# A graph network's attention: weighted rows, row maxima and a comparison counter held in PSUM

## The chip, the cores and the metric

The kernel runs as one program on one core of a Trainium2 chip. The metric is device time in microseconds (us), from start to end of one execution. Engines are named as in the profile: PE (matrix products), PEld (its weight loads), DVE (vector), ACT (scalar), POOL (which here issues indirect gathers) and SP (which issues plain transfers). SBUF is the large on-chip memory, PSUM the small one into which PE writes.

## What is computed

A node matrix x (6250 x 128) passes two residual blocks over a graph of 200,000 edges that are sorted by destination. The first block is a stack of five attention layers:

```python
def _gat_layer(x, src, dst, ea, W, We, a_src, a_dst, a_edge, b, n):
    h = x @ W
    e = ea @ We
    s = (h @ a_src)[src] + (h @ a_dst)[dst] + e @ a_edge
    s = jax.nn.leaky_relu(s, NEG_SLOPE_ATT)
    smax = jax.ops.segment_max(s, dst, num_segments=n)
    ex = jnp.exp(s - jax.lax.stop_gradient(smax)[dst])
    denom = jax.ops.segment_sum(ex, dst, num_segments=n)
    alpha = ex / denom[dst]
    out = jax.ops.segment_sum(h[src] * alpha[:, None], dst, num_segments=n)
    return out + b
...
h = jnp.maximum(_layernorm(x, axis=-1), 0.0)
x = x + _L0_gnn_ref(h, edge_index, edge_attr_16, ...)
h = jnp.maximum(_layernorm(x, axis=-1), 0.0)
x = x + _L1_gnn_ref(h, src, dst, ...)
```

Every node has a self-loop too, and between the layers there is some mixing. The second block is an edge convolution: rows of both ends of each edge are gathered, multiplied, normalised over all edges twice, and averaged per destination. The degrees of the nodes, by destination and by source, are counted as well.

## The kernel before

The edges are laid out in rows of four (K = 4) with one destination each. 128 rows make a group q; four groups (GQ = 4) make a tile of 16 columns of 128 edges. The nodes lie in 49 buckets of 128.

In order of time the kernel sorts and counts (0 to about 460 us in the profiled execution), builds edge records (L477, to about 1205), runs five attention layers (about 1259 to 14685), gathers for the edge convolution (L786, 15203 to 17639), and does the rest of that convolution.

One attention layer is `attention(l)` (L562). `heads` multiplies the nodes by the layer's weights and writes a table in HBM with a node's 128 features, a one, and its source score. Then a loop of 109 tiles calls `some`:

1. POOL issues 16 indirect gathers (L591), each of 128 table rows, into g, which has four buffers. SP loads neq (zero where a row's destination is a given node of the bucket) and eqt (the transposed match).
2. t (L602) is the gathered score plus the edge's own, tk (L604) the maximum over a row's four edges, and z (L607) is tk spread over the nodes of the bucket with a large negative number where they don't match. PE transposes z into xp (L610); tm (L611) is the maximum per node.
3. A chain of small DVE instructions (L615 to L625) makes the running maxima TS, the scores u and m, and cor, the factor by which sums so far are rescaled. `three` (L213 to L216) splits the maximum in three bf16 pieces in R6, and PE brings them back to the edge rows as me (L632); am (L634) adds the pieces up, v (L636 to L638) is the score less the maximum, and ACT's ex (L640) its exponential.
4. y is the weighted sum of a row's four gathered rows, one for each of the four groups j: ACT multiplies the first (L644) and DVE multiplies and adds the other three (L646), each reading and writing y in SBUF.
5. oh (L648, ACT) is the match. PE adds the rows of y to their nodes as op (L652), and DVE rescales the node sums hb and adds op (L655), in a bucket that is looked up in registers that `regs` loads on DVE.

In every fifth tile a step of `count` (L187) adds to the degree: two compares on DVE of a counter 0..127 with edge numbers, ol (L193) and oo (L195), and products on PE in po. It reads the counter as iotab, in bf16 in SBUF. The degree by destination is counted so in the sort too.

A Tile framework places buffers, adds the waits and decides the order of instructions within each engine's queue; the engines take their queues in order. A tile's y sums stand behind the t of two tiles later in DVE's queue. PSUM is eight banks: po takes 1, xp 2, me 2 and op 3.

Of the kernel before, what the change touches and what calls it, by code (L numbers as in the profile page):

```python
# [9 lines left out]
F32 = mybir.dt.float32  # L10
# [10 lines left out]
P = 128  # L21
# [10 lines left out]
def gnn_kernel(ctx: ExitStack, tc: tile.TileContext, x, src, dst, ea, Ws, Wes, a_srcs, a_dsts, a_edges,  # L32
# [134 lines left out]
    with tc.tile_pool(name="gat", bufs=1) as gp:  # L167
# [18 lines left out]

        def count(to, lo, hi, sw, pp, c0=0, c1=CE):  # L187

            po = pp.tile([P, NB], F32, name="po", bufs=1)
            for c in range(c0, c1, G):  # L190
                n = min(G, c1 - c)
                ol = sw.tile([P, G, P], BF, name="ol", bufs=2)
                nc.vector.tensor_tensor(ol[:, :n], mid_bc(iotab, n, P), last_bc(lo[:, c:c + n], n, P), OP.is_equal)  # L193
                oo = sw.tile([P, G, NB], BF, name="oo", bufs=2)
                nc.vector.tensor_tensor(oo[:, :n], mid_bc(iotab[:, :NB], n, NB), last_bc(hi[:, c:c + n], n, NB), OP.is_equal)  # L195
                for j in range(n):
                    nc.tensor.matmul(po, ol[:, j, :], oo[:, j, :], start=(c + j == c0), stop=(c + j == c1 - 1))
                yield
            nc.vector.tensor_tensor(to, to, po, OP.add)
# [362 lines left out]
        def attention(l):  # L562

            with tc.tile_pool(name="nod", bufs=1) as lp, tc.tile_pool(name="nodp", bufs=2, space=PSUM) as pp:
                nc.scalar.dma_start(ael[:, :K * QM], ae_d[l, :, :K * QM])
                if l:
                    heads(l, lp, pp)
                nc.vector.tensor_tensor(nod[:, 1, :], nod[:, 1, :], aeloop[:, :, l], OP.add)

                for k, to in ((0, adE), (1, t0E)):  # L570
                    tp = pp.tile([NB, P], F32, name="ntp")
                    nc.tensor.transpose(tp, nod[:, k, :], ident)
                    nT = lp.tile([NB, P], F32, name="nT", bufs=2)
                    nc.scalar.copy(nT, tp)
                    for c in range(0, Q, 512):
                        n = min(512, Q - c)
                        ps = pp.tile([P, 512], F32, name="ep")
                        nc.tensor.matmul(ps[:, :n], nT, tboh[:, c:c + n], start=True, stop=True)
                        nc.scalar.copy(to[:, c:c + n], ps[:, :n])
                rem = lp.tile([P, Q], F32, name="rem")  # L580
                three(R6[:, :, 0:3], adE, rem)
                nc.vector.memset(TS[:, 0:1], -BIG)

            with tc.tile_pool(name="edg", bufs=2) as ep, tc.tile_pool(name="edgp", bufs=2, space=PSUM) as pp:
                steps = count(outdeg, slo, shi, ep, pp, CE * l // L, CE * (l + 1) // L)

                def some(q0, n):
                    c0 = K * q0
                    g = ep.tile([P, G, HW], F32, name="g", bufs=4)
                    for j in range(G):  # L590
                        nc.gpsimd.indirect_dma_start(  # L591
                            out=g[:, j, :], out_offset=None, in_=table,
                            in_offset=bass.IndirectOffsetOnAxis(ap=srci[:, c0 + j:c0 + j + 1], axis=0))
                    neq = ep.tile([P, GQ, P], BF, name="neq", bufs=4)
                    nc.sync.dma_start(neq, neq_d[q0 // GQ])
                    eqt = ep.tile([P, GQ, P], BF, name="eqt", bufs=4)
                    nc.sync.dma_start(eqt, eqt_d[q0 // GQ])
                    r = regs(0, q0, GQ, DVE, (NB - 1) * HW)

                    t = ep.tile([P, GQ, K], F32, name="t")  # L600
                    tf = t.rearrange("p q k -> p (q k)")
                    nc.vector.tensor_tensor(tf, g[:, :, D + 1], ael[:, c0:c0 + G], OP.add)  # L602
                    tk = ep.tile([P, GQ], F32, name="tk")
                    nc.vector.tensor_reduce(tk, t, AX.X, OP.max)  # L604
                    tm = ep.tile([P, GQ], F32, name="tm")
                    z = ep.tile([P, GQ, P], F32, name="z")
                    nc.vector.scalar_tensor_tensor(z, neq, -BIG, last_bc(tk, GQ, P), op0=OP.mult, op1=OP.add)  # L607
                    xp = pp.tile([P, GQ, P], F32, name="xp", bufs=2)
                    for j in range(GQ):
                        nc.tensor.transpose(xp[:, j, :], z[:, j, :], ident)  # L610
                    nc.vector.tensor_reduce(tm, xp, AX.X, OP.max)  # L611

                    sl = slice(q0, q0 + GQ)
                    t0, ad, rst = t0E[:, sl], adE[:, sl], reset[:, sl]
                    nc.vector.tensor_tensor(tm, tm, t0, OP.max)  # L615
                    nc.vector.tensor_tensor_scan(TS[:, q0 + 1:q0 + 1 + GQ], rst, tm, TS[:, q0:q0 + 1], OP.add, OP.max)
                    u = ep.tile([P, 2, GQ], F32, name="u")
                    nc.vector.tensor_tensor(u[:, 0, :], TS[:, sl], rst, OP.add)
                    nc.vector.tensor_tensor(u[:, 0, :], u[:, 0, :], t0, OP.max)
                    nc.vector.tensor_tensor(u[:, 0, :], u[:, 0, :], ad, OP.add)  # L620
                    nc.vector.tensor_tensor(u[:, 1, :], TS[:, q0 + 1:q0 + 1 + GQ], ad, OP.add)
                    m = ep.tile([P, 2, GQ], F32, name="m")
                    nc.vector.scalar_tensor_tensor(m, u, SLOPE_ATT, u, op0=OP.mult, op1=OP.max)  # L623
                    cor = ep.tile([P, GQ], F32, name="cor")
                    nc.vector.tensor_tensor(cor, m[:, 0, :], m[:, 1, :], OP.subtract)  # L625
                    nc.scalar.activation(cor, cor, AF.Exp)
                    tmp = ep.tile([P, GQ], F32, name="tmp")
                    three(R6[:, sl, 3:6], m[:, 1, :], tmp)

                    me = pp.tile([P, GQ, 6], F32, name="me", bufs=2)  # L630
                    for j in range(GQ):
                        nc.tensor.matmul(me[:, j, :], eqt[:, j, :], R6[:, q0 + j, :], start=True, stop=True)  # L632
                    am = ep.tile([P, GQ, 2], F32, name="am")
                    nc.vector.tensor_reduce(am, me.rearrange("p g (a b) -> p g a b", b=3), AX.X, OP.add)  # L634
                    v = ep.tile([P, GQ, K], F32, name="v")
                    nc.vector.tensor_tensor(v, t, last_bc(am[:, :, 0], GQ, K), OP.add)  # L636
                    nc.vector.scalar_tensor_tensor(v, v, SLOPE_ATT, v, op0=OP.mult, op1=OP.max)
                    nc.vector.tensor_tensor(v, v, last_bc(am[:, :, 1], GQ, K), OP.subtract)  # L638
                    ex = ep.tile([P, GQ, K], F32, name="ex")
                    nc.scalar.activation(ex, v, AF.Exp)  # L640

                    y = ep.tile([P, GQ, D + 1], F32, name="y")
                    for j in range(GQ):
                        nc.scalar.activation(y[:, j, :], g[:, K * j, :D + 1], AF.Identity, bias=zeroc, scale=ex[:, j, 0:1])  # L644
                        for k in range(1, K):
                            nc.vector.scalar_tensor_tensor(y[:, j, :], g[:, K * j + k, :D + 1], ex[:, j, k:k + 1], y[:, j, :], op0=OP.mult, op1=OP.add)  # L646
                    oh = ep.tile([P, GQ, P], F32, name="oh")
                    nc.scalar.activation(oh, neq, AF.Identity, bias=onec, scale=-1.0)  # L648
                    for h in range(0, GQ, 2):
                        op = pp.tile([P, 2, D + 1], F32, name="op", bufs=3)  # L650
                        for j in (h, h + 1):
                            nc.tensor.matmul(op[:, j - h, :], oh[:, j, :], y[:, j, :], start=True, stop=True)  # L652
                        for j in (h, h + 1):
                            a = hbf[:, ds(r[j], D + 1)]
                            nc.vector.scalar_tensor_tensor(a, a, cor[:, j:j + 1], op[:, j - h, :], op0=OP.mult, op1=OP.add)  # L655

                    if q0 % (5 * GQ) == 0 and q0 < QM:
                        next(steps, None)

                over(GQ, some, lambda: nc.scalar.dma_start(ael[:, K * QM:], ae_d[l, :, K * QM:]))  # L660
                for _ in steps:
                    pass
# [304 lines left out]
```

## Time and profile before

| | us |
|---|---|
| median of 9 runs | 18727.85 (18688.21 to 18760.27) |
| profiled execution | 18761.08 |
| its span | 18759.3 |
| attention layer 0, from POOL's first gather to its last | 2579.5 |
| layer 1 | 2582.9 |
| layer 2 | 2591.1 |
| layer 3 | 2595.7 |
| layer 4 | 2597.1 |
| edge convolution's gathers | 2436 |

Between two layers' gathers lie 101 to 133 us, in which the output of the one and the table of the next are made.

The engines' busy time over the span:

```profile
PE 4505.0 (24%) x24113; PEld 3280.7 (17%) x24113; DVE 7165.9 (38%) x23773; ACT 2826.5 (15%) x5544; POOL 10656.0 (57%) x10984
```

Each entry is busy us, the share of the span, and the number of instructions. No engine is busy for more than 57% of the span. A line of a group gives the kernel's line, the engine and its operation, output and inputs, the count, then busy us and mean ns of one, then the idle time of the engine before these instructions and what ended most of it. "issue" means that nothing visible was waited for; "remote" is a wait whose releaser isn't named. A line of a timeline gives start and length in us, the instruction, and in brackets the idle time before it.

### The profile page before, as it was taken

What the parts mean: (1) busy time and instruction counts of PE and PEld (TensorE: products, weight loads), DVE (VectorE), ACT (ScalarE), POOL (GpSimd) and SP (SyncE); (2) the same over time, 40 slices, a digit from 0 to 9 for tenths busy, and PEclk for the clock granted to TensorE, in tenths of its full rate; (3) what the DMA queues carried; (4) which work ended last, traced back from release to release, by engine and by line L of the source; (5) the groups of instructions that cost most, each with busy time, mean ns of one, the idle gap of its engine ahead of it and who ended that gap; (6) DMA issues with size and microseconds to landing.
All of it is one profiled execution on the core that took longest, in us unless ns stands there. A gap on an engine that the chain in (4) does not pass through costs nothing. (4 is left out here: it accounts for less than half of the span.)

```text
span 18759.3 us, 107717 instructions
## 1 busy us (share of the span) xinstructions
PE 4505.0 (24%) x24113; PEld 3280.7 (17%) x24113; DVE 7165.9 (38%) x23773; ACT 2826.5 (15%) x5544; POOL 10656.0 (57%) x10984
## 2 busy tenths in 40 slices
PE   4111111121111221111211111211111222222498
PEld 4011111111111111111111111111111111111268
DVE  7333333343333343333433333433333421221378
ACT  1111111111111111111101111111111111111267
POOL 1657666656666556666466666566666356565300
PEclk6555555555555555555555555555555555555699
DMA  3122222222222222222222222222222222222475
GB/s 101 56 58 56 56 56 58 56 60 57 57 57 56 53 61 56 56 56 56 59 55 56 55 56 57 57 56 55 56 57 56 67 89 88 87 90 88 144 252 201
DMA packets 717072, 1361.76 MB, mean 73 GB/s; under 512 B 223808, under 2 KB 486880, under 8 KB 673632
## 3 DMA queue, kind: packets, MB, share of 16 engines
q0 software_dynamic: 348800, 702.54, 16.1%
q1 hardware_dynamic: 338828, 616.20, 10.0%
q10 hardware_dynamic: 28756, 35.62, 0.6%
q8 instruction: 215, 3.52, 0.1%
q14 instruction: 473, 3.87, 0.1%
HBM read 1144.99 MB, written 208.56 MB: 72 GB/s over the span
## 5 line engine op out<-in xcount | busy, mean ns | idle before, releaser
L591 POOL DMA_INDIRECT g<-table,srci x8720 | 8491.6, 974 | 4987.5 <-issue 4387.9
L652 PE MATMUL op<-y,oh 128*128 128x129 f32 x4360 | 1598.0, 488 | 5708.2 <-DVE y L646 4151.4
L646 DVE SCALAR_TENSOR_TENSOR y<-g,ex,y 128x129 f32<-128x129 f32 x6540 | 1954.8, 348 | 2108.1 <-DVE y L646 784.0
L786 POOL DMA_INDIRECT g<-btable,srci x1744 | 1645.3, 943 | 1309.2 <-DVE xe L800 566.9
L652 PEld LDWEIGHTS op<-y,oh 128*128 128x128 f32 x4360 | 1071.7, 314 | 6230.5 <-issue 3751.3
L648 ACT ACTIVATE oh<-neq,onesq 128x512 f32<-128x512 bf16 x545 | 392.9, 721 | 5483.1 <-PE op L652 3540.5
L655 DVE SCALAR_TENSOR_TENSOR hb<-hb,cor,op 128x129 f32 x2180 | 756.5, 347 | 1153.7 <-remote 606.2
L804 DVE COPY xs<-xps 128x512 f32<-128x512 f32 x436 | 301.3, 691 | 2202.7 <-remote 1718.4
L803 PE MATMUL xps<-ident,xe 128*128 128x128 f32 x1744 | 467.3, 422 | 2158.6 <-DVE xe L800 1710.5
L610 PE MATMUL xp<-ident,z 128*128 128x128 f32 x2180 | 594.2, 428 | 1460.1 <-DVE am L634 367.9
L644 ACT ACTIVATE y<-g,zeroc,ex 128x129 f32<-128x129 f32 x2180 | 899.3, 483 | 19.0 <-DVE m L623 0.6
L632 PE MATMUL me<-R,eqt 128*128 128x6 bf16 x2180 | 135.5, 167 | 3055.6 <-DVE tk L604 1341.9
L477 POOL DMA_INDIRECT rg<-rec_d,rowi x436 | 472.6, 1084 | 559.8 <-DVE ix L470 272.9
L640 ACT ACTIVATE ex<-v 128x16 f32<-128x16 f32 x545 | 117.5, 216 | 4365.1 <-DVE v L638 1398.4
L803 PEld LDWEIGHTS xps<-ident,xe 128*128 128x128 f32 x1744 | 307.8, 214 | 2303.6 <-issue 2284.1
L632 PEld LDWEIGHTS <-eqt 128*128 128x128 bf16 x2180 | 106.3, 105 | 3211.6 <-issue 3209.8
L610 PEld LDWEIGHTS xp<-ident,z 128*128 128x128 f32 x2180 | 389.9, 217 | 1536.1 <-issue 1331.4
L806 ACT ACTIVATE sq<-xps 128x512 f32<-128x512 f32 x436 | 260.3, 597 | 2527.2 <-DVE xs L804 2238.9
L607 DVE SCALAR_TENSOR_TENSOR z<-neq,tk 128x512 f32<-128x512 bf16 x545 | 380.5, 698 | 478.2 <-remote 299.4
L611 DVE TENSOR_REDUCE tm<-xp 128x4 f32<-128x512 f32 x545 | 374.7, 688 | 322.0 <-remote 164.6
L602 DVE TENSOR_TENSOR t<-g,ael 128x16 f32<-128x16 f32 x545 | 100.1, 184 | 840.2 <-DMA g<-table,srci 719.9
L896 PE MATMUL rps<-fs,e 128*128 128x128 f32 x3488 | 409.1, 276 | 4.6 <-ACT e L889 4.6
(315 smaller groups left out, 8241.1 us busy)
## 6 DMA issues: line engine op xcount, KB each, us to landing
g<-table,srci POOLq DMA_INDIRECT x8720
e_d<-xs SPq DMA_DIRECT2D x109, 1024.0 KB
x<-e_d SPq DMA_DIRECT2D x109, 1024.0 KB
e<-e_d SPq DMA_DIRECT2D x109, 1024.0 KB
neq<-neq_d SPq DMA_DIRECT2D x654, 128.0 KB
eqt<-eqt_d SPq DMA_DIRECT2D x654, 128.0 KB
g<-btable,srci POOLq DMA_INDIRECT x1744
table<-hb SPq DMA_DIRECT2D x5, 3185.0 KB
```

Of the source, the lines that this page charges most:

```text
L477: nc.gpsimd.indirect_dma_start(out=rg[:, j, :, :].rearrange("p k r -> p (k r)"), out_offset=None, in_=rec_d, in_offset=bass.IndirectOffset ...
L591: nc.gpsimd.indirect_dma_start(out=g[:, j, :], out_offset=None, in_=table, in_offset=bass.IndirectOffsetOnAxis(ap=srci[:, c0 + j:c0 + j + ...
L607: nc.vector.scalar_tensor_tensor(z, neq, -BIG, last_bc(tk, GQ, P), op0=OP.mult, op1=OP.add)
L610: nc.tensor.transpose(xp[:, j, :], z[:, j, :], ident)
L644: nc.scalar.activation(y[:, j, :], g[:, K * j, :D + 1], AF.Identity, bias=zeroc, scale=ex[:, j, 0:1])
L646: nc.vector.scalar_tensor_tensor(y[:, j, :], g[:, K * j + k, :D + 1], ex[:, j, k:k + 1], y[:, j, :], op0=OP.mult, op1=OP.add)
L648: nc.scalar.activation(oh, neq, AF.Identity, bias=onec, scale=-1.0)
L652: nc.tensor.matmul(op[:, j - h, :], oh[:, j, :], y[:, j, :], start=True, stop=True)
L655: nc.vector.scalar_tensor_tensor(a, a, cor[:, j:j + 1], op[:, j - h, :], op0=OP.mult, op1=OP.add)
L786: nc.gpsimd.indirect_dma_start(out=g[:, j, :], out_offset=None, in_=btable, in_offset=bass.IndirectOffsetOnAxis(ap=srci[:, c0 + j:c0 + j + ...
L803: nc.tensor.transpose(ps[:, k, :], xe[:, k, :], ident)
L896: nc.tensor.matmul(ps[:, k, :], es[:, K * q + k, :], fs, start=True, stop=True)
```

## The change

Three things that DVE and ACT read and write lie in PSUM instead of SBUF, and the eight banks are shared out anew.

- `count` copies the counter into PSUM once per call (six calls), in f32 beside po, and both compares read that copy.
- tk lies in PSUM, in one tile mt together with me. mt has one buffer; me had two, in PSUM, and tk two, in SBUF.
- The weighted rows grow in yp, a PSUM tile for two groups j with two buffers: ACT writes the first product there, DVE adds the second and third there, and the fourth step writes the sum to y in SBUF, which PE reads as before. Both groups' ACT steps come ahead of the DVE steps of the pair.
- op has two buffers instead of three. The banks are then po with the counter 1, mt 1, xp 2, yp 2 and op 2.

```diff
-            po = pp.tile([P, NB], F32, name="po", bufs=1)
+            po = pp.tile([P, 2, P], F32, name="po", bufs=1)
+
+            io, po = po[:, 0, :], po[:, 1, :NB]
+            nc.vector.tensor_copy(io, iota)
...
-                nc.vector.tensor_tensor(ol[:, :n], mid_bc(iotab, n, P), last_bc(lo[:, c:c + n], n, P), OP.is_equal)
+                nc.vector.tensor_tensor(ol[:, :n], mid_bc(io, n, P), last_bc(lo[:, c:c + n], n, P), OP.is_equal)
...
-                nc.vector.tensor_tensor(oo[:, :n], mid_bc(iotab[:, :NB], n, NB), last_bc(hi[:, c:c + n], n, NB), OP.is_equal)
+                nc.vector.tensor_tensor(oo[:, :n], mid_bc(io[:, :NB], n, NB), last_bc(hi[:, c:c + n], n, NB), OP.is_equal)
...
-                    tk = ep.tile([P, GQ], F32, name="tk")
+                    mt = pp.tile([P, GQ + 6 * GQ], F32, name="mt", bufs=1)
+                    tk = mt[:, :GQ]
...
-                    me = pp.tile([P, GQ, 6], F32, name="me", bufs=2)
+                    me = mt[:, GQ:].rearrange("p (g a) -> p g a", a=6)
...
-                    for j in range(GQ):
-                        nc.scalar.activation(y[:, j, :], g[:, K * j, :D + 1], AF.Identity, bias=zeroc, scale=ex[:, j, 0:1])
-                        for k in range(1, K):
-                            nc.vector.scalar_tensor_tensor(y[:, j, :], g[:, K * j + k, :D + 1], ex[:, j, k:k + 1], y[:, j, :], op0=OP.mult, op1=OP.add)
+                    for h in range(0, GQ, 2):
+                        yp = pp.tile([P, 2, D + 1], F32, name="yp", bufs=2)
+                        for j in (h, h + 1):
+                            nc.scalar.activation(yp[:, j - h, :], g[:, K * j, :D + 1], AF.Identity, bias=zeroc, scale=ex[:, j, 0:1])
+                        for j in (h, h + 1):
+                            for k in range(1, K):
+                                nc.vector.scalar_tensor_tensor(y[:, j, :] if k == K - 1 else yp[:, j - h, :], g[:, K * j + k, :D + 1], ex[:, j, k:k + 1],
+                                                               yp[:, j - h, :], op0=OP.mult, op1=OP.add)
...
-                        op = pp.tile([P, 2, D + 1], F32, name="op", bufs=3)
+                        op = pp.tile([P, 2, D + 1], F32, name="op", bufs=2)
```

The number of instructions per tile stays the same on each engine.

## The prediction

> **What bounds the kernel now.** I read the costliest groups first, then the windows, then the timelines. Five attention layers fill most of the span, and in each layer POOL issues 109 tiles of 16 indirect gathers (L591).
>
> ```profile
> L591 POOL DMA_INDIRECT g<-table,srci x8720 | 8491.6, 974 | 4987.5 <-issue 4387.9
> L786 POOL DMA_INDIRECT g<-btable,srci x1744 | 1645.3, 943 | 1309.2 <-DVE xe L800 566.9
> L646 DVE SCALAR_TENSOR_TENSOR y<-g,ex,y 128x129 f32<-128x129 f32 x6540 | 1954.8, 348 | 2108.1 <-DVE y L646 784.0
> L655 DVE SCALAR_TENSOR_TENSOR hb<-hb,cor,op 128x129 f32 x2180 | 756.5, 347 | 1153.7 <-remote 606.2
> ```
>
> POOL is the floor: 0.94 us of work and 0.30 us of issue make 1.25 us per gather, 20 us per tile. The layers' windows, from POOL's first gather to its last, are 2579.5, 2582.9, 2591.1, 2595.7 and 2597.1 us, 12946 us together; 8720 gathers at 1.25 us are 10900. So 2046 us lie above the floor. POOL's timeline shows what most of them are:
>
> ```profile
> 7004.81 0.94 POOL L591 DMA_INDIRECT g<-table,srci  x1 [0.30 <-issue]
> ...
> 7021.33 0.94 POOL L591 DMA_INDIRECT g<-table,srci  x1 [10.58 <-issue]
> ...
> 7025.26 1.80 POOL L591 DMA_INDIRECT g<-table,srci  x1 [0.30 <-issue]
> ...
> 7117.36 0.94 POOL L591 DMA_INDIRECT g<-table,srci  x1 [14.71 <-issue]
> ```
>
> POOL runs bursts and then stops, because the fourth buffer of g is not free: its last reader is a y sum (L646) on DVE. DVE is busy for only 8.5 us per tile (925.8 us in the second layer's window, over 109), so it is not short of work capacity; it waits. Its timeline shows how:
>
> ```profile
> 7090.66 0.17 DVE L623 SCALAR_TENSOR_TENSOR m<-u 128x8 f32<-128x8 f32 x1 [1.23 <-DVE u L620]
> 7092.07 0.16 DVE L625 TENSOR_TENSOR cor<-m 128x4 f32<-128x4 f32 x1 [1.24 <-DVE m L623]
> ...
> 7096.26 0.16 DVE L615 TENSOR_TENSOR tm<-tm,t0E 128x4 f32<-128x4 f32 x1 [1.24 <-DVE tmp L214]
> 7097.66 0.17 DVE L215 CAST R<-tmp 128x4 bf16<-128x4 f32 x1 [1.24 <-DVE tm L615]
> ...
> 7116.27 0.35 DVE L646 SCALAR_TENSOR_TENSOR y<-g,ex,y 128x129 f32<-128x129 f32 x1
> ...
> 7118.90 3.38 DVE L646 SCALAR_TENSOR_TENSOR y<-g,ex,y 128x129 f32<-128x129 f32 x12
> ...
> 7124.49 0.16 DVE L619 TENSOR_TENSOR u<-u,t0E 128x4 f32<-128x4 f32 x1
> ```
>
> For much of a burst each DVE instruction that needs the one before it starts 1.24 us after that one's end (call this the late stretch). Some 5 to 8 us after POOL stopped, it is over: the twelve y sums at 7118.90 run without a gap, the sum at 7116.27 frees the buffer, and POOL resumes 1.1 us later. In the late stretch, casts and four-element adds wait as long as the wide sums.
>
> **The change, part by part.** The sums are made against the profiled execution (18761.1 us, span 18759.3), which is 33 us (0.2%) above the median of 18727.9; I carry the differences over to the median. 0.2% is also about what a measurement of this kernel can tell from no change.
>
> *Counter in PSUM.* Six copies of 128 elements, near 0.2 us each (L602, 16 elements, takes 184 ns), are 1 us. The compares L193 and L195 take 2288 and 976 ns from a bf16 counter. L512, which compares 2048 elements with the f32 counter, takes 2282 ns. So f32 costs nothing; a PSUM operand costs nothing in L655 against L646 (347 and 348 ns, same shape). Pairs of rows of equal shape that differ in memory lie at most 14 ns apart (L800 677, L804 691), which over 2 x 97 x 2 compares is 5 us either way. I take 0.
>
> The Trainium skill ("VectorE: DVE Perf Modes", The perf-mode tier table) speaks against this part: a tensor_tensor of 2048 bf16 elements should take 1224 ns from SBUF and the single rate with any PSUM operand. By it some 194 long compares would lose 1.06 us each, 206 us of DVE time; the 2288 ns row says that nothing of the kind is there to lose.
>
> *Weighted rows in PSUM.* Twelve sums per tile stay twelve, and ACT's four stay four. DVE or ACT writing PSUM has no row in this trace; by the 14 ns above, nine writes per tile (eight sums, tk) are 0.13 us more or less, under POOL's 20 us. ACT's 483 ns (L644) may move as little. In the late stretch 14 ns vanish in waits of 1.24 us. I take 0.
>
> *POOL undisturbed.* A sum or z now reads one tensor from SBUF, not two. L591 averages 974 ns where L786, beside which no such long DVE instruction runs, averages 943: 31 ns x 8720 = 270 us. The gather at 7025.26 took 1.80 us while sums ran. The gain lies between 0 and 270. A burst that is shorter only stops sooner, since DVE frees the buffer no earlier. What stays is where POOL never stops, the first 100 to 150 us of a layer (about 5% of it, 14 us), up to everything if DVE keeps pace. I take 100.
>
> The Trainium skill ("SBUF — State Buffer", SBUF: two separate sides) has VectorE instructions with two SBUF inputs exclude a GpSimd instruction that reads SBUF for their whole length. It would give the whole 270 us back and says nothing of late DVE completions.
>
> *One buffer for row maxima and me; the order.* This is what I expect to decide. tk and me now share one PSUM tile with one buffer; before, both had two. So tk(n+1) must come after am(n), and the instructions on DVE stand otherwise. Before, with tile n's t landed, the queue holds y(n-2), then four hb updates (L655) mixed with u, tk, m, z, cor; then R's casts mixed with tm, and am, TS and v mixed with u: two tiles' chains alternate, and each fills the other's wait. After: z(n), one v step, tm(n) straight behind it (with four 428 ns transposes between), then its max, scan, y(n-1), the four hb updates mixed with u and m, then cor, the four casts, am and v of the same tile with nothing between. Counted where an instruction needs the one directly before it, or PE's answer to it: before, some 11 per tile (4 in the y sums, 3 in the updates, 4 in the rest); after, 15 (the 4 and 3 again, then tm, its max and scan, the casts 3, am, v). Gathers, SP's neq and eqt loads and PE's order are not moved; g has four buffers as before, and y still comes two landings after its gather.
>
> In the prompt stretch four more exposed steps cost little: 8.5 us of work plus the transposes (1.7) and me (0.7), in all about 11, fit in 20. In the late stretch they cost 4 x 1.24 = 5.0 us a tile. A late tile before is 11 x 1.24 + 12 = 25.6 us, after 30.6. The common cycle is two tiles (a burst of 32 gathers, 39.8 us, and a stop of 8.5 us, medians), of which 12 us after the go and the time from 5 us after the stop are prompt: about 28 us are late. These did 1.09 tiles and will do 0.91; the 0.18 missing is made up prompt, at 11 to 20 us a tile: 2.0 to 3.6 us per cycle, 1.0 to 1.8 per tile. Lower end 0: the waits for other engines hide it. Upper end 2.5 us: half of the 5.0, if the late share of the time (28 of 48) grows no shorter with longer stops. I take 1.25, since a longer stop also brings the prompt stretch: 545 x 1.25 = 681 us, with ends 0 and 1362. What is late next is the last y sum, then POOL's buffer, then t.
>
> *op's buffers from three to two.* An op needs the hb updates of the same tile; PE has 476 of 2583 us busy in a layer. 0.
>
> Sum: 0 + 0 - 100 + 681 = +581, so 18728 + 581 = 19309.
>
> **The rivals.** *The late stretch is cured (faster).* If DVE's late completions come from its own long instructions with two SBUF tensors contending with POOL's gathers, the change takes away 13 of them per tile, POOL never stops and the 2046 us go: 18728 - 2046 = 16682, or 16952 with the 270 kept. For it: the stretched gather beside the sums, and that late completions end when POOL stops. Against it: the edge convolution's gather stage has no DVE instruction of that kind (L800 reads one SBUF tensor, L804 none), yet DVE waits 30 us at a time there for PE's transposes of L800's result (each 422 ns, L803), late again while POOL gathers:
>
> ```profile
> 16529.04 0.68 DVE L800 TENSOR_TENSOR xe<-g,ar 128x512 f32<-128x512 f32 x1
> 16560.25 0.69 DVE L804 COPY xs<-xps 128x512 f32<-128x512 f32 x1 [30.53 <-remote]
> ```
>
> And the 1.24 us is the same behind a cast, a scan or a sum. It decides from where it takes away over 581/2046 = 28% of the excess, the 100 being counted already.
>
> *Partly cured.* Fewer or shorter late stretches: half of 2046 gone and the order's half price kept is -1023 + 340 = -683, about 18045.
>
> *Nothing moves.* Late completions go by number of instructions, which doesn't change; the added steps hide behind the remote waits (299 us before z, 606 before the updates), and POOL gains nothing since it stops anyway: 18728.
>
> *The added steps fall late at full price*, 4 x 1.24 in every tile: 545 x 5.0 = 2700, so 21430. Against it: stops lengthen and bring prompt stretches.
>
> **How the numbers follow.** Forecast (slower, own range 18770 to 20100): 0.53. Full price, above 20100: 0.07. Nothing moves: 0.06. Partly cured, 17100 to 18690: 0.18. Cured, 16400 to 17100: 0.16, of which about 0.06 below 16650. So faster 0.34, same 0.06, slower 0.60. 19310 is the forecast's value. The range must reach to the cure to leave out no more than 2 in 10: 16650 to 20100 leaves 0.13.
>
> **What would show it.** Right: L591's mean falls towards 943, y's sums stay near 348 ns and ACT's near 483, DVE's chain still starts 1.24 us apart in bursts, POOL's idle time (4987.5) grows, windows of about 2650 to 2750 us per layer, and the waits before tm, R's casts and am grow. Wrong: windows near 2180 us with POOL unbroken (cure); windows of 2590 us (nothing moves); or PSUM sums dearer than 400 ns, which would add a term I set at 0.

## The result and the profile after

The changed kernel takes 18836.28 us (median of 10 runs, 18805.76 to 18862.88) against 18722.89 us before in the same measurement: a ratio of 1.0059, interval 1.005 to 1.0069. It is 113 us slower; 581 had been forecast. Its profiled execution has a span of 18839.2 us, 80 us more than before.

The changed kernel's costliest groups, in the same columns as before's:

```profile
L594 POOL DMA_INDIRECT g<-table,srci x8720 | 8234.4, 944 | 5232.1 <-issue 4635.4
...
L653 DVE SCALAR_TENSOR_TENSOR yp<-g,ex,yp 128x129 f32<-128x129 f32 x4360 | 1338.6, 352 | 1484.1 <-DVE yp L653 707.0
...
L663 DVE SCALAR_TENSOR_TENSOR hb<-hb,cor,op 128x129 f32 x2180 | 760.3, 349 | 921.0 <-PE op L660 416.4
...
L653 DVE SCALAR_TENSOR_TENSOR y<-g,ex,yp 128x129 f32<-128x129 f32 x2180 | 697.7, 346 | 556.1 <-DVE y L653 339.6
L650 ACT ACTIVATE yp<-g,zeroc,ex 128x129 f32<-128x129 f32 x2180 | 879.8, 448 | 18.6
```

A gather went from 974 to 944 ns, which is 257 us less of POOL's busy time (8491.6 to 8234.4). But the idle time in front of the gathers went from 4987.5 to 5232.1 us, 245 more. DVE's sums cost what they did (352 and 346 ns for 348), and ACT's write to PSUM takes 448 ns for 483.

The windows of the five layers, from POOL's first gather to its last (length, then busy us of PE, PEld, DVE, ACT and POOL with their instructions, then the granted clock of PE, the share of the DMA engines and GB/s; the first and the last layer are shown):

```profile
1359.20:3957.50 2598.30, 443.22 (x1976) 312.59 (x1975) 962.81 (x3852) 293.44 (x743) 1646.77 (x1744) 0.50 0.23 56
...
12186.40:14771.90 2585.50, 446.59 (x1969) 313.72 (x1969) 965.00 (x3872) 292.87 (x744) 1646.76 (x1744) 0.50 0.23 56
```

The five together are 12920 us, 26 less than before (12946): in the layers neither the 257 us saved nor the 681 us feared arrived. The loss lies ahead of them. The first layer starts at 1359.2 us, not at 1259.7, because the first record gather (L477 before, L480 after) starts at 549.9 us, not at 446.9. The sort's degree count shows why. DVE's timeline, before:

```profile
249.01 2.29 DVE L193 TENSOR_TENSOR ol<-iotab,dlo 128x2048 bf16<-128x2048 bf16 x1
251.22 0.97 DVE L195 TENSOR_TENSOR oo<-iotab,dhi 128x784 bf16<-128x784 bf16 x1
252.10 2.29 DVE L193 TENSOR_TENSOR ol<-iotab,dlo 128x2048 bf16<-128x2048 bf16 x1
```

and after:

```profile
251.67 2.29 DVE L196 TENSOR_TENSOR ol<-po,dlo 128x2048 bf16<-128x2048 f32 x1 [0.91 <-PE po L200]
253.88 0.96 DVE L198 TENSOR_TENSOR oo<-po,dhi 128x784 bf16<-128x784 f32 x1
255.76 2.29 DVE L196 TENSOR_TENSOR ol<-po,dlo 128x2048 bf16<-128x2048 f32 x1 [0.92 <-PE po L200]
```

The compares are as long as before, but each pair now takes 4.09 us instead of 3.09: ol waits 0.91 us for PE's products of the pair before. The profile names its input po: the counter's copy and the counts are two halves of one PSUM tile, and the wait is for the tile. 98 pairs at 1.0 us are 98 of the 103 us by which the first record gather is late.

### The profile page after: what moved, and what is told of

Its sections match the earlier page's. It is cut to its first block, busy times and chain, and to the rows that moved or that the text cites. A ratio compares the mean times of both kernels' runs of the same rounds, so it can differ in the third digit from the quotient of the medians.

```text
span 18839.2 us, 108293 instructions
## 1 busy us (share of the span) xinstructions
PE 4395.1 (23%) x24113; PEld 3258.0 (17%) x24113; DVE 7279.7 (39%) x23779; ACT 2813.0 (15%) x5544; POOL 10371.5 (55%) x10984
## 5 line engine op out<-in xcount | busy, mean ns | idle before, releaser
L594 POOL DMA_INDIRECT g<-table,srci x8720 | 8234.4, 944 | 5232.1 <-issue 4635.4
L660 PE MATMUL op<-y,oh 128*128 128x129 f32 x4360 | 1471.2, 474 | 4766.1 <-DVE y L653 2908.4
L653 DVE SCALAR_TENSOR_TENSOR yp<-g,ex,yp 128x129 f32<-128x129 f32 x4360 | 1338.6, 352 | 1484.1 <-DVE yp L653 707.0
L812 DVE COPY xs<-xps 128x512 f32<-128x512 f32 x436 | 301.5, 692 | 2191.7 <-remote 1682.8
L653 DVE SCALAR_TENSOR_TENSOR y<-g,ex,yp 128x129 f32<-128x129 f32 x2180 | 697.7, 346 | 556.1 <-DVE y L653 339.6
L650 ACT ACTIVATE yp<-g,zeroc,ex 128x129 f32<-128x129 f32 x2180 | 879.8, 448 | 18.6
L480 POOL DMA_INDIRECT rg<-rec_d,rowi x436 | 472.9, 1085 | 654.0 <-DVE ix L473 371.4
L636 PE MATMUL mt<-R,eqt 128*128 128x6 bf16 x2180 | 135.1, 167 | 2867.6 <-DVE R L219 2317.2
L200 PE MATMUL po<-oo,ol 128*128 128x49 bf16 x3126 | 167.6, 217 | 1062.5 <-DVE oo L198 736.8
```

The lines of the kernel that those rows point to most:

```text
L480: nc.gpsimd.indirect_dma_start(out=rg[:, j, :, :].rearrange("p k r -> p (k r)"), out_offset=None, in_=rec_d, in_offset=bass.IndirectOffset ...
L594: nc.gpsimd.indirect_dma_start(out=g[:, j, :], out_offset=None, in_=table, in_offset=bass.IndirectOffsetOnAxis(ap=srci[:, c0 + j:c0 + j + ...
L650: nc.scalar.activation(yp[:, j - h, :], g[:, K * j, :D + 1], AF.Identity, bias=zeroc, scale=ex[:, j, 0:1])
L653: nc.vector.scalar_tensor_tensor(y[:, j, :] if k == K - 1 else yp[:, j - h, :], g[:, K * j + k, :D + 1], ex[:, j, k:k + 1], yp[:, j - h, : ...
```

## The experiments

**Which part of the change costs.** Four kernels on one chip, where the kernel before took 18739.73 us:

- a_counter_sbuf: the change without the counter's lines; `ol` and `oo` read `iotab` and po stands alone.
- b_counter_only: before, with the counter's lines alone.
- b_mt_only: before, with `tk = mt[:, :GQ]` and `me = mt[:, GQ:]` in a tile of one buffer.
- b_y_only: before, with yp; to make room `me ... bufs=1` and `op ... bufs=2`.

The layers' figures in this and the next tables are of one profiled execution each; whole executions of one kernel lie up to 125 us apart on this chip.

> The changed kernel with the counter part alone undone (bf16 counter in SBUF, po by itself). Theory A (the added wait): in the changed kernel the counter's copy lies in the same PSUM tile that PE's products fill, so each compare waits for the products of the compare before; that cost is the sort's longer start, 103 us of the profiled execution, and all else of the change is near nothing. It expects the sort back at about 447 us before the first record gather, and about 18735 us in all, within 0.3% of the kernel before. Rival B (the attention layers cost it): the time stays near 18830.

> The kernel before with the counter part alone. Theory A: about 18825 us, the sort 100 us longer, layers as before (2580 to 2597 us). Rival B: about 18730 us.

> The kernel before with tk and me in one PSUM tile of one buffer, nothing else; DVE's order in a tile becomes the serial one of the changed kernel. Theory A: the layers' sum within 30 us of 12946. Rival C (two terms of opposite sign cancel in the changed kernel: the serial order costs several hundred us, undisturbed POOL gives them back): layers' sum up by 200 to 680 us, 18930 to 19400 in all, POOL's gathers still 974 ns.

> The kernel before with the weighted rows growing in PSUM alone (me with one buffer, op with two, to make room). Theory A: POOL's gathers fall to about 945 ns, its stops grow by as much, layers' sum within 30 us of 12946. Rival C: stops stay as they were, the layers give 200 to 270 us, 18450 to 18530 in all.

| | us | ratio to before | first record gather | layers together | a gather |
|---|---|---|---|---|---|
| a_counter_sbuf | 18650.05 | 0.9948 (0.9928 to 0.9967) | 448.8 us | 12868 us | 962 ns |
| b_counter_only | 18928.03 | 1.0105 (1.0083 to 1.0128) | 549.7 | 13003 | 958 |
| b_mt_only | 18781.64 | 1.0019 (1.0007 to 1.0031) | 448.4 | 12929 | 977 |
| b_y_only | 18797.73 | 1.0032 (1.0021 to 1.0042) | 447.7 | 12944 | 961 |

The counter costs 188 us alone (18928 - 18740) and some 200 in company: each against its own measurement of before, the change is 113 us slower and the change without the counter 90 us faster. 100 of it are in the sort and, in these single executions, 52 to 57 in the layers. So theory A had the sort right, but not the total of either kernel (18735 and 18825), and why the counter costs in the layers stays open. Without the counter the change is 0.5% faster. The two other parts cost 42 and 58 us alone and gain 90 together; that they don't add up isn't explained. b_y_only's gathers fell to 961 ns, not to 945: the compares keep their share, as b_counter_only, which relieves the compares alone, shows with 958.

Rival C falls, though b_mt_only by itself doesn't settle it. Its layers stay where they were (-18 us), but its order is not quite that of the change: max and scan are mixed with the hb updates behind the y sums, where the change has them straight behind tm. a_counter_sbuf has the change's own order on DVE. POOL's busy time is 102 us less there (8389.1 for 8491.6), and the layers are 78 us shorter. If all 102 came through and nothing else gained, the order cost some 24 us, not several hundred.

How the serial order could be free is seen in b_mt_only's POOL timeline (the gathers between, 0.30 us apart, left out):

```profile
7014.99 0.94 POOL L591 DMA_INDIRECT g<-table,srci  x1 [10.77 <-issue]
...
7085.58 0.94 POOL L591 DMA_INDIRECT g<-table,srci  x1 [9.80 <-issue]
...
7158.09 0.95 POOL L591 DMA_INDIRECT g<-table,srci  x1 [12.26 <-issue]
```

From go to go are 70.6 and 72.5 us: bursts of 48 gathers now (164 of its 177 bursts have just 48, counting as a stop what lasts over 3 us), three tiles to a stop of 10.7 us (median), where before the median burst had 32 and the stop 8.4. I counted as late the runs of over 4 us in which DVE's instructions that need another of DVE's start over 0.4 us after its end: by several ways to cut such a run off, they are 0.50 to 0.61 of the layers' time before and 0.40 to 0.50 here. Here the cycle shifted instead of stretching. The change itself shifted otherwise: its median burst still has 32 gathers, with more stops (291 for 225) that are shorter (6.1 us for 8.4).

**Shared tile or PSUM itself.** f_io_own is the kernel before with the counter in PSUM, in a tile of its own; to make room, op has two buffers and the sort's cp takes a buffer of bp. Its edit against before, cut to the counter and op:

```diff
             po = pp.tile([P, NB], F32, name="po", bufs=1)
+            io = pp.tile([P, P], F32, name="io", bufs=1)
+            nc.vector.tensor_copy(io, iota)
...
-                        op = pp.tile([P, 2, D + 1], F32, name="op", bufs=3)
+                        op = pp.tile([P, 2, D + 1], F32, name="op", bufs=2)
```

> The kernel before with the counter in PSUM, but in a tile of its own (to make room, op has two buffers and the sort's one-off cp uses the tile of bp). Theory A (the shared tile makes each compare wait for the products before it): the sort is short again, about 447 us, and the time is within 0.3% of before. Rival D (reading the counter from PSUM is what costs): the sort stays at about 550 us and the time near 18930 us.

18796.71 us against 18712.46, ratio 1.0037 (1.0019 to 1.0055). The first record gather is back at 455.1 us, so the shared tile was the cause in the sort. The total just missed its bound: the layers took 13020 us, with op's third buffer gone too. b_counter_only has all three buffers of op and 13003, so the counter in PSUM is the likelier cause; it was not tried apart.

**Is DVE's number of completions the pace?** d_extra8 and d_sig4 are a_counter_sbuf with additions, z_act16 and z_pe16 the kernel before. d_extra8 adds eight small copies on DVE per tile, `nc.vector.tensor_copy(spare[:, j:j + 1], tf[:, j:j + 1])`; d_sig4 adds four, each read by an `nc.scalar.copy`. z_act16 takes sums away: `for c in range(G): nc.scalar.activation(yk[:, c, :], g[:, c, :D + 1], ...)` and two `tensor_reduce`. z_pe16 gives the 16 rows of yk to PE, four accumulating products per group.

> The changed kernel with the counter in SBUF, and eight one-column DVE copies more per tile, which nobody waits for, at a place where DVE waits for PE's transposes anyway. They are some 0.6 us of DVE time. Theory E1 (late completions go one by one, about 1.4 us each, whoever waits): 8 x 1.4 us x the late share (0.5 to 0.75) = 6 to 8 us a tile, 3000 to 4500 us more. Theory E2 (a completion is delayed for those that wait, without a queue): under 0.6 us a tile, below 300 us more.

> The changed kernel with the counter in SBUF, and four one-column DVE copies more per tile, each read by an ACT copy, so that each of them must be signalled on its own; 0.3 us of DVE work and 0.8 us of ACT work per tile. Theory E1: four completions more per tile at about 1.2 us in the late stretch (half of the time), 2.4 us a tile, some 1300 us more (all four late: 2600). Rival E3: as the eight unsignalled copies had it or less, under 400 us more.

> The kernel before, with all 16 weighted rows of a tile made by ACT (16 multiplications instead of 4) into an SBUF tile and summed by two DVE reductions instead of twelve DVE sums; nothing in PSUM. DVE has ten signalling instructions fewer per tile, 26 for 36, and some 1 us less work. Theory E1 (in the late stretch DVE's completions are passed on at about one per 1.2 us, whatever depends on them; the layers' pace is the number of DVE completions): the late stretch holds 6261 of 19205 completions now, so ten fewer per tile (5450) take nearly all of it away; layers' sum near 11000 to 11400, 16800 to 17200 us in all. Rival E3 (POOL's gathers keep DVE late for a share of the time, whatever DVE does): layers' sum stays above 12500.

> The same, but PE adds the 16 weighted rows up (16 products op of 488 ns in place of 4, 7.8 us of PE a tile) and DVE has no sum at all: 24 signalling instructions for 36. Theory E1: layers' sum 10900 to 11300, about 16700 to 17100 us in all, unless the late stretch moves to PE, which then has the most to do, as in the edge convolution. Rival E3: above 12500.

| | us | ratio to before | layers together |
|---|---|---|---|
| d_extra8 | 19066.32 | 1.0185 (1.0168 to 1.0202) | 13245 us |
| d_sig4 | 18843.51 | 1.0048 (1.0031 to 1.0066) | 12979 |
| z_act16 | 19208.28 | 1.0238 (1.0214 to 1.0261) | 13301 |
| z_pe16 | 20163.16 | 1.0752 (1.0726 to 1.0777) | 14330 |

Theory E1 falls. Four signalled completions more cost 111 us in the layers against a_counter_sbuf, not 1300, and ten or twelve fewer made the kernel slower. (That they are slower says less by itself: both also give ACT 12 more products of 488 ns per tile, and z_act16 spares DVE nothing, with 8.7 us of work per tile for 8.6, since each of its reductions takes 1.91 us. d_extra8 says less than meant: its 4360 copies raise the semaphore 1025 times, about twice a tile. Its 377 us are 0.69 us a tile, about the 0.75 us that the copies take.) Where the lateness went in z_pe16, its timeline shows:

```profile
7016.53 0.25 PE L632 MATMUL me<-R,eqt 128*128 128x6 bf16 x4 [10.74 <-issue]
...
7033.95 0.94 POOL L591 DMA_INDIRECT g<-table,srci  x1 [0.30 <-issue]
...
7040.42 0.18 DVE L634 TENSOR_REDUCE am<-me 128x8 f32<-128x24 f32 x1 [24.04 <-remote]
...
7048.42 0.95 POOL L591 DMA_INDIRECT g<-table,srci  x1 [13.52 <-ACT yk L645]
```

PE's four products me are done by 7017; DVE, which waits for nothing else, goes on at 7040.42, 6.5 us after POOL began its last gather. The trace has the change of PE's semaphore for these products only at 7040.40. With DVE relieved it is PE whose completions come late, as in the edge convolution. They are late while POOL gathers without a break, and come through soon after it stops. z_act16 points the same way: DVE waits 2626 us before the hb updates and 1969 before tm, both of which read PE's results, for a releaser that isn't named, against 606 and 165 in the kernel before.

**Breaks in POOL's gathers.** A memset of a piece of g ahead of a gather (`nc.gpsimd.memset(g[:, j, :w], 0.0)`, overwritten by the gather) slows POOL; the queue orders them in groups. p_pace4 has one ahead of every fourth gather, p_pace1 one of 64 elements ahead of each, both on a_counter_sbuf.

> The changed kernel with the counter in SBUF, and on POOL a small memset of g ahead of every fourth gather, so that POOL spends more time per tile. Theory E (attention's pace of about 23.6 us a tile is DVE's, through its late completions; POOL's own speed doesn't matter): bursts are slower and stops shorter, the layers' sum stays within 60 us of 12868. Rival F (POOL's pace matters too, any added POOL time is added to the layers): some 0.4 us x 4 x 545 = 870 us more. Rival G (the late stretches come from gathers issued at 1.25 us and go when they are slower): layers fall towards POOL's new floor, about 21.5 us a tile, 1100 us less.

> The same with a memset ahead of every gather, POOL at some 1.5 us a gather, near the mean it reaches now (1.48). Theory E: POOL hardly stops, DVE still falls late while POOL works, layers' sum within 200 us of 12868. Rival F: stops stay and the memsets are added, 16 x 0.25 x 545 = 2200 us more. Rival G: late stretches are gone, DVE waits for gathers, POOL unbroken at its floor.

p_pace4: 19033.47 us, 1.0164 (1.0147 to 1.0181), layers 13226, 358 us more than a_counter_sbuf. Within a burst four gathers and the break take 5.08 us for 5.00, which is 0.32 us a tile or 174 us; F's 870, E's 60 and G's gain are all missed. p_pace1: 18405.25 us, 0.9835 (0.9818 to 0.9851), layers 12599. POOL was made slower and the kernel faster. POOL's timeline of p_pace1:

```profile
7014.48 0.95 POOL L593 DMA_INDIRECT g<-table,srci  x1 [0.16 <-issue]
7015.74 0.94 POOL L593 DMA_INDIRECT g<-table,srci  x1 [0.30 <-issue]
7016.99 0.95 POOL L593 DMA_INDIRECT g<-table,srci  x1 [0.30 <-issue]
7017.94 0.34 POOL L592 MEMSET g<- 128x64 f32 x3
7018.44 0.95 POOL L593 DMA_INDIRECT g<-table,srci  x1 [0.16 <-POOL g L592]
```

Three gathers and a break come to 3.96 us, and DVE's late share, by the same ways to count, is 0.15 to 0.31 for 0.33 to 0.52 in a_counter_sbuf, lower by each of them. No theory had this by its numbers: E's bound was 200 us and it was 269.

**The dose, and a surprise.** p_w16, p_w130 and p_2x vary the memsets; p_b64 puts p_pace1's in the kernel before.

> The same with a memset of 16 elements ahead of every gather; the queue then holds them in groups of seven and nine, so POOL breaks for about 0.7 us after seven or nine gathers. Theory S with a reset (a short break before the tenth gather keeps completions prompt): late share below 0.3, layers 11600 to 12200. Theory S without a reset (breaks only let some completions through): late share 0.4 to 0.5 and layers 12700 to 13100.

> The changed kernel with the counter in SBUF, and a memset of a whole column of g ahead of every gather; POOL's queue then holds two memsets, two gathers, and so on. Theory S (completions of another engine are starved while gathers follow each other unbroken, and get through in POOL's breaks): DVE's late share falls below 0.2, POOL hardly stops, and the layers come to POOL's own floor, about 2.95 us per two gathers, 23.6 us a tile, layers' sum about 12850. Rival F (POOL's time is simply added to the stops): late share near 0.5 and 14800.

> The same with two half-column memsets ahead of every gather, four between two pairs of gathers. Theory S: late share below 0.1, no stops, the layers at POOL's floor of about 3.2 us per two gathers, 25.6 us a tile, 13950 in all for the layers. Rival F: above 15000.

> The kernel before with a half-column memset ahead of every gather, as in p_pace1 but with none of the change. Theory S: the layers fall from 12946 to 12600 to 12750, about 18450 us in all. If the PSUM rows are needed for it: 18700 or more.

On the chip that took these four the kernel before needs 16466.21 us, not some 18730. p_w16 is at 1.0098 (1.0081 to 1.0115) of that, p_b64 at 1.0318 (1.0301 to 1.0335), p_w130 at 1.0513 (1.0495 to 1.053), p_2x at 1.0661 (1.0644 to 1.0679). In none of the four traces does POOL stop for over 3 us within a layer. So here nothing is late, and the breaks only cost: layers 11383, 11806, 12123 and 12372 us in that order. As tests of the dose the four were lost; what they showed is that the lateness comes with the chip, or its condition at the time; the kernel alone doesn't bring it about.

**The change where nothing is late.** The last three, on yet another chip; the kernel before took 16484.85 us. r_own is the change with a counter tile of its own in the sort, r_sbuf is a_counter_sbuf.

> The changed kernel again. If before takes about 16466 us here (a chip without late completions, POOL unbroken at its floor): the sort costs 100 us more, the gathers' mean falls from about 974 to 944 ns and that is now worth its full 30 ns x 8720 = 260 us, so about 16300 us, 1.0% faster than before. If before takes about 18730: 18840, as shown.

> The changed kernel with the sort's copy of the counter in a PSUM tile of its own (cp uses bp's tile to make room), layers as in the change. The sort's added wait is gone: 100 us less than r_after on either chip, 16200 or 18740 us.

> The changed kernel with the counter in SBUF everywhere. Sort short; the compares read two SBUF tensors again, so gathers beside them are stretched (mean 962 ns, as in a_counter_sbuf). If before is 16466: 18 ns x 8720 = 155 us more than r_own in the layers, about 16350. If before is 18730: 18650, as shown.

| | us | ratio to before | first record gather | layers together | a gather |
|---|---|---|---|---|---|
| r_after (the change) | 16200.09 | 0.9828 (0.9815 to 0.9842) | 550.3 us | 10883 us | 943 ns |
| r_own | 16107.47 | 0.9771 (0.9758 to 0.9784) | 454.5 | 10883 | 943 |
| r_sbuf | 16249.86 | 0.9858 (0.9843 to 0.9873) | 447.4 | 11026 | 960 |

There the same change is 1.7% faster. Each of the three took some 100 us less than expected, and about as much of the change's gain can't be placed (see the next section). The gathers' group and the first and last windows in r_after:

```profile
L594 POOL DMA_INDIRECT g<-table,srci x8720 | 8227.3, 943 | 3200.0 <-issue 2614.5
```

```profile
1331.50:3508.00 2176.50, 416.29 (x1968) 307.23 (x1968) 892.64 (x3873) 295.11 (x746) 1645.06 (x1744) 0.50 0.27 66
...
10528.60:12705.40 2176.80, 416.96 (x1969) 307.73 (x1969) 902.68 (x3872) 292.86 (x744) 1645.32 (x1744) 0.50 0.27 66
```

Each layer is POOL's floor, 1744 gathers at 1.248 us, and DVE finishes a tile's work and waits for the next tile, in r_after's DVE timeline:

```profile
7007.21 0.17 DVE L641 SCALAR_TENSOR_TENSOR v<-v 128x16 f32<-128x16 f32 x1
7017.11 0.18 DVE L605 TENSOR_TENSOR t<-g,ael 128x16 f32<-128x16 f32 x1 [9.72 <-DMA g<-table,srci]
```

The counter has two effects that can be told apart here: its shared tile costs 93 us (16200 - 16107), and reading it from PSUM gains 142 (16250 - 16107), since the compares no longer stretch the gathers beside them (960 to 943 ns).

## Why the prediction was wrong

**The counter, taken as 0.** The price was right (2284 ns for 2281 over the sort's 98 long compares); the wait was missed. I read the halves of one tile as two things, and never asked what else is written in the tile that a compare reads. That is the 100 us of the sort, and nearly the whole measured difference of 113. So it is luck that the time moved the way that was forecast and fell inside the forecast's own range: the layers, from which the loss was to come, gained 26 us.

**POOL undisturbed, 0 to 270, taken as 100.** The mechanism was right: 974 to 944 ns. On a chip with late completions no worth of it is seen, as its sentence "a burst that is shorter only stops sooner" said: POOL's stops of over 3 us grew from 1825 to 2088 us while its busy time fell by 257. Where POOL never stops, it comes through: the compares' part, 16 ns a gather, is worth 142 us between r_sbuf and r_own, and the change gained 285 us, the sort's 93 to the bad. (That is 378 us outside the sort. Some 270 are the gathers, if before's take 974 ns there as p_b64's do on the other undisturbed chip. The rest, about 110, can't be placed, as no trace of the kernel before was taken there; it is also what the three expectations missed.) The Trainium skill ("SBUF — State Buffer", SBUF: two separate sides) lets a VectorE instruction with two SBUF inputs shut out a GpSimd instruction that reads SBUF for its length; 943 ns without such long instructions, 960 with the compares alone and 974 with all agree with it.

**One buffer for row maxima, +681.** This step failed. I priced four exposed waits at 1.24 us each, with a late stretch of 28 us in every cycle of two tiles. The new order did expose waits, as those before tm show, first before, then after:

```profile
L611 DVE TENSOR_REDUCE tm<-xp 128x4 f32<-128x512 f32 x545 | 374.7, 688 | 322.0 <-remote 164.6
L615 DVE TENSOR_REDUCE tm<-xp 128x4 f32<-128x512 f32 x545 | 376.8, 691 | 1001.0 <-issue 628.3
```

But they were not added to the layers. b_mt_only, with an order close to it and nothing else, gave -18 us there, and a_counter_sbuf, with the change's own order, leaves some 24 us for it, if POOL's saving came through whole and nothing else gained. The wrong part is the overlap: I held the cycle of two tiles fixed, so that more exposed waits could only lengthen it. The cycle moved, to bursts of 48 gathers in b_mt_only and to more and shorter stops in the change. (By the prediction's own bounds the late part is nearer 33 us than 28: 39.8 and 8.5, less 12 and 3.5. That would have made the term larger, not smaller.) On the undisturbed chip DVE waits 9.7 us per tile for the next gathers (5306.6 us over 545 tiles), and that covers the order whole.

**PSUM operands at 0** and the sums' 348 ns: right, 346 to 352; but the counter's 52 to 57 us in the layers of the first chips stay unexplained. **op's two buffers at 0**: not tried alone.

**The rivals.** The cure did not come from the change, and the argument against it, that the edge convolution is late with no DVE instruction of that kind, held: z_pe16 shows PE late in the layers too. But the time that I gave to a cure, 16682 to 16952, is not far above what two other chips take for the kernel before (16466 and 16485). The late stretches that I read as the kernel's habit came with the chip or the hour.

## What to carry to other kernels

Two values that share a tile share its waits: ask of every operand moved into an occupied tile who else writes there, since the price of the instruction will not show it. An engine's saving counts only where that engine sets the pace, so look at what its stops are waiting for before adding it up. And where completions are seen late with no cause in the kernel, run the kernel before on a second chip: here the same change loses 0.6% on one and gains 1.7% on another.

## What the runs showed of the hardware

On the first chips completions came late while POOL issued indirect gathers without a break. What is late is the change of the semaphore, not the start behind it. In the layers of the kernel before, a quarter of DVE's 4679 waits for its own instructions found the semaphore changed 1.02 us or more after the instruction's end, and the next began some 22 ns after that; in r_after 95 in 100 of 5326 found it changed within 11 ns. The record of the changes is thinner too: DVE's instructions raise its semaphore 23659 times in the kernel before, and the trace has 16885 changes; in r_after it has 23681 of 23704. PE and ACT have 3854 of 5431 and 2894 of 5113 before, and all but three at most in r_after. Whether several arrive as one or some go unrecorded, the trace doesn't tell.

With the changed kernel the first completion of DVE's that is over 0.4 us late comes 12.2 us, or 10 gathers, after POOL resumed (median of the 267 bursts that have one, half of them between 11.0 and 14.1 us, some near 1 us), and the last 5.4 us after it stopped (median). The engine whose late completions are waited for was DVE in the layers, PE in the edge convolution and, with DVE's sums taken over, in the layers as well.

On two other chips the same kernels had none of it: the waits of the copy behind PE in the edge convolution (L804 before, L812 after) fell from 2202.7 to 554.2 us, the convolution's gathers from 2728 to 2177 us. (2728 us is all 1744 of them, from 14912.2; the 2436 us of the table ahead start at 15203 and have 1551.) One chip of the first kind gave 18712 and 18747 us for the kernel before, 19 minutes apart. Each of the other two was measured once, and after all of the first kind; so whether it is the chip or the hour was not settled, nor what holds a completion back. PE's granted clock doesn't tell the kinds apart: it is 0.538 in the changed kernel's profile on the first and 0.542 on the second. The best version differs too: a_counter_sbuf with p_pace1's breaks on the first kind, r_own on the second; r_own was not run on the first kind, and breaks like p_pace1's cost 521 us on the second.
